# The third linear block turned by transfers and VectorE instead of TensorE, and three norms moved, in a two-layer sequence kernel on one Trainium2 core

## The chip, the cores and the metric

The kernel runs on one core of one Trainium2 chip. The metric is device time in microseconds (us) for one launch; lower is better. The kernel before takes 1119.91 us (median of three runs, 1119.85 to 1121.25). All times inside the run come from one profiled execution, which took 1119.75 us; its instructions span 1118.0 us. Engines have short names in the profile: PE is TensorE's matmuls, PEld its weight loads, DVE is VectorE, ACT ScalarE, POOL GpSimd, SP SyncE, which issues nearly all DMAs here. L770 is line 770 of the kernel before.

## The reference: what is computed

The input is 2 sequences of 1024 tokens, 512 wide. Four stages follow, each of the form "x = layernorm(x + f(x))" where f is, in turn, a Mamba layer (a selective state space with a short convolution and a gated RMS norm), a linear layer with ternary weights whose rows are rescaled by their norms, an RG-LRU (a gated linear recurrence with a short convolution), and a gated feed-forward network (SwiGLU) with integer weights. The two stages at which the change works come down to this:

```
# linear layer (L0_ffn)
out = einsum('bln,nk->blk', x, weight) * scale          # weight in {-1, 0, 1}
v   = max(norm(out), 1e-7)
out = out * tanh(v) / (v + 1e-7)
out = out * min(0.99 / max(norm(out), 1e-7), 1)

# RG-LRU (L1_attn)
y  = gelu(x @ w_y + b_y)
xb = x @ w_x + b_x
conv = conv_b + sum_k conv_w[k] * shift(xb, K - 1 - k)
gate_x, gate_a = sigmoid(conv @ w_ig + b_ig), sigmoid(conv @ w_ag + b_ag)
h = scan(exp(-8 * gate_a * softplus(a_param)), gate_x * conv * sqrt(1 - a * a))
out = (h * y) @ w_out + b_out
```

## The kernel before

**Tiling.** The 2048 tokens are four blocks of 512 tokens (block 0 to block 3, two to a sequence). A block's rows lie in X[b], 128 partitions by 4 rows of 512. A matmul needs its input with the features on the partitions, "turned". Two ways of turning are in the code:
- `transposed` (L226) does it on TensorE: for each of four feature pieces four transposes into one PSUM bank (L237), then a copy to SBUF. With `split` the copy is ScalarE's cast to a shorter float type (L241), and VectorE subtracts it from the original (L244), so that two matmuls on fast types give the exact product.
- `load_blocks` and `turn_blocks` (L260, L270) do it without TensorE: the rows are read back from DRAM by four DMAs that place 32 by 32 squares (256 KB each, in pieces of 128 bytes), and VectorE turns the squares in place, four instructions of 128x512 (L273). `split` (L939) then makes the two pieces, ScalarE's cast at L942 and VectorE's subtraction at L944.

**Stages on the time axis.** The Mamba layer runs over blocks 0 to 3 until about 450 us, the linear layer's blocks stand around 440 to 510 us, the RG-LRU follows to about 757, the feed-forward network to 1109, and the tail ends at 1118.

**Order of the work.** Stages are Python generators, and `weave` (L303) takes steps of a second generator between steps of the first by a written plan. `weave(branches(0, st), linear(2), (1,) * 4)` (L1174) thus mixes the first RG-LRU block's branch with the third linear block. The order on each engine follows from the emission and from a scheduler that may move instructions; `keep_in_program_order` and `high_priority` pin or hasten some, and `manual_schedule` fixes the tail as written. Each engine runs its queue strictly in that order.

**Mamba norms.** `conclude(b)` (L763) computes block b's output product (po, L770), adds it to the rows (L785), normalises them with `layernorm` (statistics L283 and L286 on VectorE, square root on ScalarE L288, reciprocal L289, then subtract and multiply L291 on VectorE or on GpSimd) and stores them to x_mid[b] in DRAM (`store_rows`, L257). conclude(b) is woven into block b+1's `project` and `recur` (L795 to L830). In recur, VectorE's scans (L578) produce what TensorE needs next.

**Linear layer.** `linear(b)` (L955): turned pieces, then for each of four row groups j a bank po of eight matmuls (L974), scaled on VectorE (L978), squared on ScalarE (L980), then a dozen operations on 128x4 elements (L984 to L996), the update of X[b] (L998, four instructions), and a `layernorm` on GpSimd with a store to x_lin[b]. Blocks 0 to 2 are turned by TensorE. Block 3 is turned from `mid`, which L1049 loads from x_mid[3]; the same block of code also loads X[3] and, in linear(3), the weights w14 of the RG-LRU's output.

**RG-LRU branch.** `branches(b)` (L1062): the turned block, then four channel groups m, each a product p (L1056) on TensorE, a padded copy xpad whose first three columns GpSimd clears (memset, L1079) or fills from the block before (L1081), ScalarE's bias add (L1082), VectorE's convolution (L1085 and three taps, L298); then four products for y with ScalarE's Gelu (L1093). xpad has two buffers, so channel group 2 waits for the convolution of group 0. `gates` (L1097) follows with eight more products.

**Tail.** The last block's four row groups are added up, normalised and stored one by one (L1305 to L1333). Row group 2 is normalised by two ScalarE passes (L1361, L1362) and stored from ScalarE's queue; row group 3 takes VectorE's statistics (L1364), a root on ScalarE (L1366), and is stored from SP.

Of the kernel before, what the change touches and what calls it, by code (L numbers as in the profile page):

```python
# [9 lines left out]
F32 = mybir.dt.float32  # L10
# [27 lines left out]
def model_kernel(ctx: ExitStack, tc: tile.TileContext, t: dict, out: bass.AP):  # L38
# [184 lines left out]
        nc.vector.tensor_scalar(r, z, 0.0, None, ALU.max)  # L223
        nc.vector.scalar_tensor_tensor(o, p, 2.0, r, ALU.mult, ALU.add)

    def transposed(pool, b, X, tags=("xT",), split=False, bufs=1, by_act=False, behind=False, soon=False):  # L226


        pieces = [
            pool.tile([P, NK, TB], F32R if split else F32, tag=tag, name=f"{tag}{b}", bufs=bufs)  # L230
            for tag in tags
        ]
        xT = pieces[0]
        for k in range(NK):
            pt = bank("pt")
            for j in range(NJ):
                nc.tensor.transpose(  # L237
                    pt[:, j * P : (j + 1) * P], X[b][:, j, k * P : (k + 1) * P], ident
                )
            if split:  # L240
                copied = nc.scalar.copy(xT[:, k, :], pt)  # L241
                if behind:
                    tc.keep_in_program_order(copied)
                nc.vector.tensor_tensor(  # L244
                    pieces[1][:, k, :], pt, xT[:, k, :].bitcast(F32), ALU.subtract
                )
            elif soon:
                with tc.high_priority():
                    nc.scalar.copy(xT[:, k, :], pt)
            elif k % 2 or by_act:  # L250
                nc.scalar.copy(xT[:, k, :], pt)
            else:
                nc.vector.tensor_copy(xT[:, k, :], pt)
        return pieces

    def store_rows(rows, x):
        nc.sync.dma_start(rows.rearrange("(j p) d -> p j d", p=P), x)  # L257
# [46 lines left out]
    def weave(main, fill, plan, rest=True):  # L304

        for i, _ in enumerate(main):
            for _ in range(plan[i] if i < len(plan) else 0):
                next(fill, None)
        for _ in fill if rest else ():
            pass  # L310
# [451 lines left out]
    def conclude(b, st):  # L762


        xc, sums = st["xc"], st["sums"]
        rms = sp.tile([P, NJ], F32, tag="rms", name="rms")
        for j in range(NJ):
            po = bank("po")
            for m in range(NX):
                nc.tensor.matmul(  # L770
                    po, xc[:, m, j * P : (j + 1) * P], w_out[:, m, :],
                    start=(m == 0), stop=(m == NX - 1),
                )
                if m == NX // 2 - 1:
                    yield
            if j == 0:
                pss = bank("pss")
                for i in range(NJ):
                    nc.tensor.matmul(
                        pss[:, i : i + 1], sums[:, i * P : (i + 1) * P], ones,  # L780
                        start=True, stop=True,
                    )
                nc.scalar.activation(rms, pss[:, :NJ], AF.Sqrt, bias=eps, scale=1.0 / DI)
                nc.vector.reciprocal(rms, rms)
            nc.vector.scalar_tensor_tensor(  # L785
                X[b][:, j, :], po, rms[:, j : j + 1], X[b][:, j, :], ALU.mult, ALU.add
            )
            yield
        layernorm(X[b])
        store_rows(x_mid[b], X[b])  # L790

    def by_blocks(b, st):

# [14 lines left out]
    for b in range(NBLK):  # L808
        if b:
            g, coming = gates(b, st), {}  # L810
            fill, plan = conclude(b - 1, before), (0, 0, 2, 0, 2, 0, 2, 2)
            ahead = iter(())
            if b + 1 < NBLK:
                by_blocks(b + 1, coming)
                ahead = head(b + 1, coming)
            weave(project(b, st), fill, plan, rest=False)

            weave(recur(b, H, st), alternate(itertools.chain(fill, g), ahead), (3,) * NJ)
        else:
            turns = (ahead, g, ahead, g, g, g, ahead)  # L820
            weave(recur(b, H, st), (next(steps, None) for steps in turns), (2, 2, 1, 2))
            for m in range(NX):
                tc.keep_in_program_order(nc.gpsimd.tensor_scalar(
                    w_out[:, m, :], w_out[:, m, :], normw[:, m : m + 1], 1.0, ALU.mult, ALU.mult
                ))
        H = st["H"]
        gate(b, st)
        before, st = st, coming
# [43 lines left out]
    def later_layers(exact, last=None):  # L872
# [82 lines left out]
        def linear(b):  # L955

            tags = ("wu0", "wd0") if exact else ("wu0",)
            if b == NBLK - 1:
                turn_blocks(mid)
                w1.append(wp.tile([P, NK, D], F32, tag="w4", name="w14" + suffix))  # L960
                xT = [ep.tile([P, NK, TB], WT, tag=tag, name=f"{tag}{b}") for tag in tags]
                split(mid, xT)
                nc.sync.dma_start(w1[4], w_sources["w_out"])
            else:

                xT = transposed(ep, b, X, tags=tags, split=exact, behind=b == 2)
            yield
            o = ep.tile([P, NJ, D], F32, tag="wF", name="o" + suffix)
            ssq = sp.tile([P, NJ], F32, tag="ssq", name="ssq")
            for j in range(NJ):  # L970
                po = bank("po")
                for k in range(NK):
                    for x in xT:
                        nc.tensor.matmul(  # L974
                            po, x[:, k, j * P : (j + 1) * P], wf[:, k, :],
                            start=(k == 0 and x is xT[0]), stop=(k == NK - 1 and x is xT[-1]),
                        )
                nc.vector.tensor_tensor(o[:, j, :], po, f0s, ALU.mult)  # L978
                junk = ep.tile([P, GW], mybir.dt.bfloat16, tag="junk", name="junk2")
                nc.scalar.activation(junk, o[:, j, :], AF.Square, accum_out=ssq[:, j : j + 1])  # L980
                if j % 2:
                    yield
            norm = sp.tile([P, NJ], F32, tag="norm", name="norm")
            nc.scalar.activation(norm, ssq, AF.Sqrt)  # L984
            v = sp.tile([P, NJ], F32, tag="v", name="v")
            nc.vector.tensor_scalar(v, norm, 1e-7, None, ALU.max)
            f = sp.tile([P, NJ], F32, tag="f", name="f")
            nc.scalar.activation(f, v, AF.Tanh)
            nc.vector.tensor_scalar(v, v, 1e-7, None, ALU.add)
            nc.vector.reciprocal(v, v)  # L990
            nc.vector.tensor_tensor(f, f, v, ALU.mult)
            nc.vector.tensor_tensor(norm, norm, f, ALU.mult)
            nc.vector.tensor_scalar(norm, norm, 1e-7, None, ALU.max)
            nc.vector.reciprocal(norm, norm)
            nc.vector.tensor_scalar(norm, norm, 0.99, 1.0, ALU.mult, ALU.min)
            nc.vector.tensor_tensor(f, f, norm, ALU.mult)  # L996
            for j in range(NJ):
                nc.vector.scalar_tensor_tensor(  # L998
                    X[b][:, j, :], o[:, j, :], f[:, j : j + 1], X[b][:, j, :],
                    ALU.mult, ALU.add,  # L1000
                )
            layernorm(X[b], engine=nc.gpsimd, last=None if b else nc.vector)
            if b:
                store_rows(x_lin[b], X[b])
            yield
# [39 lines left out]
        with tc.tile_pool(name="rec" + suffix, bufs=1, side="right", reuse_waits="tile") as rp:  # L1045
            carry = rp.tile([P, NK, 3], F32, tag="carry", name="carry1")
            last_h = rp.tile([P, NK], F32, tag="last", name="last")

            mid = rp.tile([P, NK, TB], F32, tag="xT", name="mid" + suffix)  # L1049
            load_blocks(mid, x_mid[3])  # L1050
            nc.sync.dma_start(X[3], rows_mid[3])

            def product(i, m, rhs):
# [117 lines left out]
                yield  # L1171

            st = {}
            weave(branches(0, st), linear(2), (1,) * 4)  # L1174
            lin = [coming_block(1)]
            bout = row("L1_attn_b_out", D, c1, nc.sync, "scale")
            ys = []
# [35 lines left out]
        with tc.tile_pool(name="ffn" + suffix, bufs=1, side="right", reuse_waits="tile") as fp:  # L1213
# [50 lines left out]
            for b in range(NBLK):  # L1264
# [29 lines left out]
                if final:  # L1294
# [37 lines left out]
                    def store(j, engine):  # L1332
                        engine.dma_start(xout[b][:, j, :], X[b][:, j, :])  # L1333
# [9 lines left out]
                    with tc.manual_schedule(  # L1343
# [13 lines left out]
                                store(j - 1, nc.sync)  # L1357
                        row_sum(3, False)
                        inverse(2)
                        x = X[b][:, 2, :]  # L1360
                        nc.scalar.activation(x, x, AF.Identity, bias=off[:, 2])  # L1361
                        nc.scalar.activation(x, x, AF.Identity, scale=rs[:, 2])  # L1362
                        row_st = sp.tile([P, 6], F32, tag="st", name="stf", bufs=4)
                        nc.vector.bn_stats(row_st, X[b][:, 3, :])  # L1364
                        nc.vector.bn_aggr(mean[:, 3, :], row_st)
                        nc.scalar.activation(rs[:, 3], mean[:, 3, 1:2], AF.Sqrt, bias=eps)  # L1366
                        store(2, nc.scalar)
                        inverse(3)
                        normed(3, nc.vector, mean[:, 3, 0:1], ALU.subtract)
                        store(3, nc.sync)  # L1370
                else:
                    for j in range(NJ):
                        r = fp.tile([P, D], F32, tag="r", name="r2", bufs=2)
# [60 lines left out]
```

## Time and profile before

| what | value |
|---|---|
| median of three runs | 1119.91 us (1119.85 to 1121.25) |
| profiled execution | 1119.75 us |
| its span | 1118.0 us |
| mean granted TensorE clock | 0.997 |
| 32 transposes, blocks 0 and 2 (L237, 458.27 to 461.76) | 3.49 us |
| one product of the RG-LRU (L1056) | 3.44 us |
| one normalisation on GpSimd, with subtraction (L291) | mean 2.17 us, 19 of them |
| one normalisation on VectorE (L291) | mean 0.57 us, 41 of them |
| four turns on VectorE (L273, 493.04) | 2.46 us |
| store of a block's rows to x_mid, issue to landing | 4.3 us (median) |

How to read it: the busy line gives for each engine its busy time, the share of the span and the number of instructions. A line of the waits gives an engine, its operation and line, what it waited for, and then the total, the number of times and the longest. A line of a timeline gives start, length, engine, line, operation, output and inputs, size and count, and in brackets the idle time before it with what ended it. Matmuls overlap, so their lengths are longer than their distance; the time of a group is read from start to the next start.

### The profile page before, as it was taken

The page shows a single profiled execution, that of the slowest core. Times are in us where ns is not written, and L with a number is a line of the kernel's source. Part 1 is how long each engine was busy: PE and PEld are TensorE (multiplying, and loading weights), DVE is VectorE, ACT ScalarE, POOL GpSimd, SP SyncE. Part 2 cuts the span into 40 slices and gives each one's busy share as a digit, 9 for nine tenths or more (in the row PEclk, how much of TensorE's full clock was granted, in tenths as well). Part 3 has the DMA queues.
Part 4 walks back from the last instruction along what each step waited for, and adds up shares of the span by engine and source line. Part 5 has one row for each costly group of instructions (what it writes and reads, how often), then busy time and mean ns, then how long its engine had stood idle before and what let it go on. Part 6 is the DMA issues. An engine that isn't in the chain of part 4 may idle for free.

```text
span 1118.0 us, 12076 instructions
## 1 busy us (share of the span) xinstructions
PE 1099.4 (98%) x4450; PEld 663.6 (59%) x4450; DVE 704.4 (63%) x1267; ACT 452.7 (40%) x692; POOL 364.5 (33%) x346
## 2 busy tenths in 40 slices
PE   9999999999999999999999999999999999999996
PEld 5455445445544555745444444447888888888885
DVE  5989797697869676874647438184238865325224
ACT  3334633463454233466654372553233224224223
POOL 1546471465248340273533231236411001001000
PEclk9999999999999999999999999999999999999998
DMA  8004202801220138336550001204654002100001
GB/s 323 21 9 122 94 1 92 207 0 38 88 98 0 39 124 226 67 94 153 111 76 25 13 1 44 32 0 138 192 95 76 1 1 62 15 1 32 6 1 41
DMA packets 122059, 77.04 MB, mean 69 GB/s; under 512 B 94512, under 2 KB 95312, under 8 KB 120456
## 3 DMA queue, kind: packets, MB, share of 16 engines
q1 hardware_dynamic: 120792, 75.77, 25.6%
q8 instruction: 37, 0.61, 0.2%
q10 hardware_dynamic: 976, 0.39, 0.1%
q14 instruction: 30, 0.25, 0.1%
q0 software_dynamic: 224, 0.02, 0.0%
HBM read 59.95 MB, written 16.02 MB: 68 GB/s over the span
## 4 chain that ended last, share of the span: by engine, by line
PE 81%; DVE 11%; ACT 4%; issue 1%; POOL 1%; DMA 1%; SPq 0%; DVEq 0%; ACTq 0%; POOLq 0%
PE pgu L1026 20%; PE p L1056 19%; PE po L1257 10%; PE pg L372 9%; PE px L372 7%; PE po L770 4%; DVE acc L298 3%; PE po L1146 2%; PE py L705 2%; PE po L974 2%; DVE L L578 2%; PE pxt L674 1%; PE pt L237 1%; DVE st L283 1%; POOL x L1152 1%
## 5 line engine op out<-in xcount | busy, mean ns | idle before, releaser
L1037 DVE SCALAR_TENSOR_TENSOR h<-pgu,L_ffn_up_scale,sg 128x512 f32<-128x512 f32 x63 | 47.1, 748 | 126.6 <-PE pgu L1026 122.8
L770 PE MATMUL po<-w_out,xc 128*128 128x512 f32 x256 | 112.5, 593 | 2.8 <-DVE L L578 2.8
L372 PE MATMUL px<-xT,w_in 128*128 128x512 f32 x256 | 114.6, 597 | 0.0
L593 POOL TENSOR_TENSOR L<-L,gm 128x512 f32<-128x512 f32 x64 | 93.4, 1490 | 64.8 <-DVE bdec L588 38.3
L372 PE MATMUL pg<-xT,w_in 128*128 128x512 f32 x256 | 113.5, 594 | 0.0
L1056 PE MATMUL p<-cv,w 128*128 128x512 f32 x256 | 110.8, 592 | 0.0
L1026 PE MATMUL pgu<-wF__4239,wg 128*128 128x512 f32 x256 | 101.7, 397 | 0.0
L1026 PE MATMUL pgu<-lo__4240,wg 128*128 128x512 f32 x256 | 100.8, 394 | 0.0
L1026 PE MATMUL pgu<-lo__4240,wu 128*128 128x512 f32 x256 | 100.7, 393 | 0.0
L1026 PE MATMUL pgu<-wF__4239,wu 128*128 128x512 f32 x256 | 100.7, 393 | 0.0
L1257 PE MATMUL po<-wd,hh 128*128 128x512 f32 x252 | 98.2, 396 | 0.3 <-POOL wg L917 0.3
L1257 PE MATMUL po<-wd,hl 128*128 128x512 f32 x252 | 98.2, 396 | 0.2 <-DVE hl L1041 0.2
L1036 ACT ACTIVATE sg<-pgu,L_ffn_gate_scale 128x512 f32<-128x512 f32 x63 | 43.4, 688 | 127.7 <-PE pgu L1026 127.6
L770 PEld LDWEIGHTS po<-w_out,xc 128*128 128x128 f32 x256 | 48.4, 190 | 63.8 <-issue 56.2
L1040 ACT CAST hh<-h 128x512 fp32r<-128x512 f32 x63 | 39.1, 620 | 112.5 <-DVE h L1037 112.3
L1056 PEld LDWEIGHTS p<-cv,w 128*128 128x128 f32 x256 | 48.6, 190 | 60.4 <-issue 59.1
L1056 PE MATMUL p<-xT,w 128*128 128x512 f32 x192 | 82.9, 592 | 0.0
L372 PEld LDWEIGHTS px<-xT,w_in 128*128 128x128 f32 x256 | 47.5, 190 | 57.5 <-issue 56.0
L372 PEld LDWEIGHTS pg<-xT,w_in 128*128 128x128 f32 x256 | 47.3, 190 | 54.2 <-issue 53.3
L1375 POOL TENSOR_TENSOR x<-x,r 128x512 f32<-128x512 f32 x12 | 15.1, 1291 | 195.2 <-DVE r L1374 195.2
L298 DVE SCALAR_TENSOR_TENSOR acc<-xpad,cols,acc 128x512 f32<-128x512 f32 x72 | 67.0, 933 | 18.5 <-ACT acc L342 13.8
L578 DVE TENSOR_TENSOR_SCAN L<-pl,id 128x512 f32<-128x512 f32 x64 | 74.9, 1205 | 4.5 <-ACT pl L572 3.5
(294 smaller groups left out, 1926.1 us busy)
## 6 DMA issues: line engine op xcount, KB each, us to landing
L<-decays SPq DMA_DIRECT2D x12, 1024.0 KB, 7.3
x_mid<-x SPq DMA_DIRECT2D x4, 1024.0 KB, 4.3
x<-x_mid SPq DMA_DIRECT2D x4, 1024.0 KB, 7.9
st<-in_L_ffn_gate_w_dram SPq DMA_DIRECT2D x8, 512.0 KB, 5.8
st<-in_L_ffn_up_w_dram SPq DMA_DIRECT2D x8, 512.0 KB, 4.1
st<-in_L_ffn_down_w_dram SPq DMA_DIRECT2D x8, 512.0 KB, 3.7
x_rec<-x SPq DMA_DIRECT2D x4, 1024.0 KB, 4.7
x<-_attn_hidden_states_dram SPq DMA_DIRECT2D x3, 1024.0 KB
```

Source lines behind the costliest of these rows:

```text
L298: tap = nc.vector.scalar_tensor_tensor(acc, xpad[:, k : k + TB], w[:, k : k + 1], acc, ALU.mult, ALU.add)
L372: nc.tensor.matmul(pm[:n, :], w_in[:, k, lo : lo + n], xT[:, k, :], start=(k == 0), stop=(k == NK - 1),)
L578: nc.vector.tensor_tensor_scan(L[:, h, :], pl, id4.rearrange("p j t -> p (j t)"), 0.0, ALU.mult, ALU.add)
L593: nc.gpsimd.tensor_tensor(L[:, h, :], L[:, h, :], st["gm"], ALU.mult)
L705: nc.tensor.matmul(pys[i][hh * HD : (hh + 1) * HD, q, :], dtx[q][:, 2 * i + hh, :], L[:, h, s], start=(first and q == 0), stop=(q == 1), s ...
L770: nc.tensor.matmul(po, xc[:, m, j * P : (j + 1) * P], w_out[:, m, :], start=(m == 0), stop=(m == NX - 1),)
L1026: nc.tensor.matmul(pm, w[g][:, k, cols], x[:, k, :], start=(k == 0 and x is pieces[0]), stop=(k == NK - 1 and x is pieces[-1]),)
L1036: nc.scalar.activation(sg, pgu[0], AF.Silu, scale=gs[:, m : m + 1])
L1037: nc.vector.scalar_tensor_tensor(h, pgu[1], us[:, m : m + 1], sg, ALU.mult, ALU.mult)
L1040: nc.scalar.copy(halves[0], h)
L1056: nc.tensor.matmul(pm, w1[i][:, k, m * P : (m + 1) * P], rhs[:, k, :], start=(k == 0), stop=(k == NK - 1),)
L1257: nc.tensor.matmul(po[j], x[:, j * P : (j + 1) * P], wd[m // GK][:, m % GK, :], start=(m == 0 and x is h[0]), stop=(m == NF - 1 and x is h ...
```

## The change

The diff has three parts.

1. linear(2) no longer uses `transposed`: like block 3 it is read back from x_mid[2] by four DMAs, turned by VectorE and split from SBUF. Both loads (mid[2] and mid[3]) are issued with high priority, and in the changed program's order their eight DMAs follow the store of x_mid[3] on SP. mid[2] takes a buffer of the tag "y". The weave's plan becomes (0, 0, 0, 0, 1, 0, 1, 1), so linear(2) starts after four steps more of branches(0), and the load of w14 moves from linear(3) to behind that weave.
2. Block 0's norm and store are taken out of conclude(0) and put into block 1's recur at its third chunk, with pinned statistics (`first_norm`, new). The last block's statistics are pinned too.
3. In the tail, row group 2 is normalised by one GpSimd instruction and stored from SP, and row group 3 is stored from ScalarE's queue.

```diff
             if split:
-                copied = nc.scalar.copy(xT[:, k, :], pt)
-                if behind:
-                    tc.keep_in_program_order(copied)
+                nc.scalar.copy(xT[:, k, :], pt)
...
-        layernorm(X[b])
-        store_rows(x_mid[b], X[b])
+        if b:
+            layernorm(X[b], pinned=b == NBLK - 1)
+            store_rows(x_mid[b], X[b])
+
+    def first_norm(chunks):
+
+
+        for c, _ in enumerate(chunks):
+            if c == 2:
+                layernorm(X[0], pinned=True)
+                store_rows(x_mid[0], X[0])
+            yield
...
-            weave(recur(b, H, st), alternate(itertools.chain(fill, g), ahead), (3,) * NJ)
+            chunks = recur(b, H, st)
+            if b == 1:
+                chunks = first_norm(chunks)
+            weave(chunks, alternate(itertools.chain(fill, g), ahead), (3,) * NJ)
...
-            if b == NBLK - 1:
-                turn_blocks(mid)
-                w1.append(wp.tile([P, NK, D], F32, tag="w4", name="w14" + suffix))
+            if b > 1:
+                turn_blocks(mid[b])
                 xT = [ep.tile([P, NK, TB], WT, tag=tag, name=f"{tag}{b}") for tag in tags]
-                split(mid, xT)
-                nc.sync.dma_start(w1[4], w_sources["w_out"])
+                split(mid[b], xT)
             else:
-
-                xT = transposed(ep, b, X, tags=tags, split=exact, behind=b == 2)
+                xT = transposed(ep, b, X, tags=tags, split=exact)
...
-            mid = rp.tile([P, NK, TB], F32, tag="xT", name="mid" + suffix)
-            load_blocks(mid, x_mid[3])
+            mid = {}
+            for b, tag, bufs in ((2, "y", 2), (3, "xT", 1)):
+                mid[b] = rp.tile([P, NK, TB], F32, tag=tag, name=f"mid{b}{suffix}", bufs=bufs)
+                with tc.high_priority():
+                    load_blocks(mid[b], x_mid[b])
             nc.sync.dma_start(X[3], rows_mid[3])
...
-            weave(branches(0, st), linear(2), (1,) * 4)
+            weave(branches(0, st), linear(2), (0, 0, 0, 0, 1, 0, 1, 1))
+            w1.append(wp.tile([P, NK, D], F32, tag="w4", name="w14" + suffix))
+            nc.sync.dma_start(w1[4], w_sources["w_out"])
...
-                        x = X[b][:, 2, :]
-                        nc.scalar.activation(x, x, AF.Identity, bias=off[:, 2])
-                        nc.scalar.activation(x, x, AF.Identity, scale=rs[:, 2])
+                        normed(2, nc.gpsimd, off[:, 2], ALU.add)
+                        store(2, nc.sync)
...
-                        store(2, nc.scalar)
                         inverse(3)
                         normed(3, nc.vector, mean[:, 3, 0:1], ALU.subtract)
-                        store(3, nc.sync)
+                        store(3, nc.scalar)
```

## The prediction

> **What bounds the kernel now.** I read the busy times first, then TensorE's list of waits, then the timelines of TensorE, VectorE, GpSimd and ScalarE from 444 to 505 us, and last the two other places that the change touches (134 to 145, 190 to 202, and the tail from 1108). Columns of a wait: us in total, times, longest.
>
> ```profile
> PE 1099.4 (98%) x4450; PEld 663.6 (59%) x4450; DVE 704.4 (63%) x1267; ACT 452.7 (40%) x692; POOL 364.5 (33%) x346
> ```
>
> ```profile
> PE po L770 <- DVE L L578: 2.8, 2, 1.9
> ...
> PE po L974 <- DVE wd L244: 0.8, 1, 0.8
> ```
>
> TensorE works 98% of the span and its waits add up to some 9 us, nearly all before 460. So whatever TensorE no longer does is gained in full, and any new wait is lost in full: behind it nothing has slack to give back (after 515 us its waits are 0.3 and 0.2). Two of the listed waits lie where the change works: 1.9 of the 2.8 at 143 us, and the 0.8 in the second block's linear product.
>
> **Part 1, the mamba norms.** Timeline of VectorE, then TensorE, in block 1 (start, length, engine):
>
> ```profile
> 137.11 0.68 DVE L283 BATCH_NORM_STATS2 st<-x 128x6 f32<-128x512 f32 x1
> 137.83 0.18 DVE L286 BATCH_NORM_AGGREGATE mv<-st 128x2 f32<-128x6 f32 x1
> 137.93 0.72 DVE L785 SCALAR_TENSOR_TENSOR x<-po,rms,x 128x512 f32<-128x512 f32 x1
> 138.68 0.69 DVE L283 BATCH_NORM_STATS2 st<-x 128x6 f32<-128x512 f32 x1
> 139.41 0.18 DVE L286 BATCH_NORM_AGGREGATE mv<-st 128x2 f32<-128x6 f32 x1
> 139.50 4.54 DVE L578 TENSOR_TENSOR_SCAN L<-pl,id 128x512 f32<-128x512 f32 x4
> ```
>
> ```profile
> 142.99 3.27 PE L770 MATMUL po<-w_out,xc 128*128 128x512 f32 x7 [1.95 <-DVE L L578]
> ```
>
> Block 0's statistics stand right ahead of the scans (L578) that TensorE then waits for. Two pairs of 0.82 leave that chain: 1.5 to 1.64 of the 1.95 go. They come back at 193 us, where VectorE stands idle for 3.51 us until 196.86. Four pairs (3.28) fit in; the reciprocal, two ScalarE table loads and four normalisations (1.95 us by the row at 456) do not all, and delay the gate chain from 198.18 by an estimated 1.15. VectorE then works without a gap from 226.6 to 258 and meets TensorE at 264.4 with about 0.3 to spare, so most of it is lost there. Net: −0.35 (ends −1.6, delay hidden, and +0.7, nothing won at 143). Two queues move with it: on SP the first store goes behind block 1's decays, and a load of block 3's rows behind it; no one waits for either before 240 us.
>
> The pinned statistics of the last block leave the place ahead of linear(1)'s subtractions (two of 0.67, at 449.14 and 449.80), and TensorE's wait of 0.79 at 451.74 goes, with about 0.2 of first-operand pacing: −0.97. Their cost comes later: block 3's rows are normalised at about 462.4 instead of 457.7, and the store follows.
>
> **Part 2, the transposes.** TensorE around linear(2):
>
> ```profile
> 458.27 3.65 PE L237 MATMUL pt<-ident,x 128*128 128x128 f32 x32
> 461.76 3.60 PE L1056 MATMUL p<-w,w 128*128 128x512 f32 x8
> ...
> 475.94 20.76 PE L1056 MATMUL p<-w,w 128*128 128x512 f32 x48
> ```
>
> 32 transposes take 3.49 us from start to start; half go: −1.75. A product of the recurrence takes 3.44 (20.6 us for 6). In the changed order six of them stand ahead of linear(2), so TensorE reaches linear(2) at 457.3 (linear(1)'s end) + 1.75 + 6 × 3.44 = 479.7, on the old clock.
>
> When is its operand there? It is now turned by VectorE, and the changed program puts those turns behind the convolutions of the first RG-LRU block and behind the turns of block 3. The convolutions' last two channels wait for a GpSimd memset (L1079), and in the new order both memsets stand behind linear(1)'s four normalisations; before, one stood ahead:
>
> ```profile
> 475.36 0.10 POOL L1079 MEMSET xpad<- 128x3 f32 x1 [1.40 <-DVE cv L298]
> 476.08 8.95 POOL L291 TENSOR_SCALAR x<-x,mv,rs 128x512 f32<-128x512 f32 x4 [0.62 <-DVE rs L289]
> 484.98 0.10 POOL L1079 MEMSET xpad<- 128x3 f32 x1
> ```
>
> and on VectorE (update, reciprocal, turns):
>
> ```profile
> 467.94 2.73 DVE L998 SCALAR_TENSOR_TENSOR x<-o,f,x 128x512 f32<-128x512 f32 x4
> ...
> 475.75 0.17 DVE L289 RECIPROCAL rs<-rs 128x4 f32<-128x4 f32 x1
> ...
> 493.04 2.46 DVE L273 STREAM_TRANSPOSE mid<-mid 128x512 f32<-128x512 f32 x4
> ```
>
> Step by step, with rows of before: ScalarE's four copies of block 0 end 2.65 behind 457.3; root (0.3), reciprocal and block 3's four normalisations (1.95) end at 462.4; linear(1)'s dozen small operations at 464.5; its update (2.73) at 467.2; four statistics pairs and the first convolution step at 470.5; table load 1.28, root and reciprocal, behind three taps, at 473.1. GpSimd: 4 × 2.07 (the shortest such row; VectorE then stands idle) to 481.4. Two convolutions (seven operations of about 0.68) to 486.2, block 3's turns (2.46) to 488.7, linear(2)'s first turn (0.62) and its cast (0.6) to 490.0. The subtractions wait for all four turns (491.1) and end at 493.9. TensorE by then has done 9 of linear(2)'s first 16 half-products (2.05) and a quarter of a product (0.86), and would have done so by 482.5: **stall 11.4**. The bounds: if the operations between take the shortest rows and taps overlap better, 8; with GpSimd at the 2.24 of the row above and transfers late by 2 us, 14.
>
> The transfers come second. All eight stand on SP behind block 3's store (4.3 us from issue to its completion by the rows of before), so they start at about 466.8. Before, 0.75 MB of such loads moved in 6.3 us (120 KB/us) and 1 MB of the later ones in 7 (140): 2 MB are there between 482 and 484, before VectorE gets to them. By themselves they would hold TensorE for 5 to 7 us.
>
> A GpSimd row is worth a second look: the same engine normalises in 0.77 in the tail where the first operation is an addition:
>
> ```profile
> 1109.36 0.77 POOL L1328 TENSOR_SCALAR x<-x,off,rsf 128x512 f32<-128x512 f32 x1 [0.72 <-DVE rsf L1325]
> ```
>
> The Trainium skill (GPSIMD Engine Reference, 3.1 Elementwise) counts 1.8 cycles an element at best, 769 ns for 512 elements. That agrees with L1328 and not with L291's 2.07 to 2.35, which stand for every normalisation that subtracts; by the page's figure the stall would be 5.2 shorter, about 6.
>
> **What an idle TensorE costs afterwards.** No row of before shows it idle for 10 us. The nearest is its own start: the 24 matmuls from 1.43 to 6.35, of the transposes' form, take 205 ns each where the later ones take 109.
>
> ```profile
> 1.43 4.92 PE L188 MATMUL early<-ident 128*128 128x128 f32 x24 [1.43 <-POOL ident masks.py:199]
> ```
>
> If it is slow again after the stall, the 2.7 us of work available from 490.1 to 493.9 need 2.7 × 205/109 = 5.1, which is 1.3 more than there is. Bounds: 0 and 24 × 96 ns = 2.3. I take 1.3, by the only row in which TensorE starts from idle.
>
> The Trainium skill (TensorE: Matmul & The Clock Gate, What's actually happening) says that the clock halves after an idle window of about 3.4 us and comes back after as much sustained work. By it the loss would be about 1.7, an estimate; the first rows agree in kind, though their column of the granted clock shows 1.00.
>
> **What follows the stall.** Everything later moves back by 8 to 9 us with TensorE. Linear(3)'s pieces are made while TensorE does the products in between; the gates' chain of block 1 needs GpSimd's squares, which by the rows end some 9 us ahead of need. I count nothing.
>
> **Part 3, the tail.**
>
> ```profile
> 1110.50 0.71 ACT L1361 ACTIVATE x<-x,off 128x512 f32<-128x512 f32 x1
> ...
> 1111.24 0.72 ACT L1362 ACTIVATE x<-x,rsf 128x512 f32<-128x512 f32 x1
> 1111.86 0.28 ACT L1366 ACTIVATE rsf<-mvf,eps 128x1 f32<-128x1 f32 x1
> ```
>
> The last row's root waits for ScalarE's two passes. The aggregate ends at 1111.61, so without them the root starts at 1111.63: −0.23. GpSimd's pass (0.77) ends at about 1111.6, beside this chain. The last store goes to ScalarE's queue: −0.25 in all (ends −0.5 and +0.2).
>
> **Sum**, against the profiled execution's 1119.75 (0.16 below the median of the runs shown, so nothing is corrected): −0.35 − 0.97 − 1.75 − 0.25 = −3.32, and + 11.4 + 1.3: **1129.1**.
>
> **Rivals.**
> A, the forecast: GpSimd's normalisations hold the convolutions, these hold the turns, TensorE stalls 10 to 13 us. For it: the waits of the changed program and the row of 8.95. 0.64; 1126 to 1131.
> B: GpSimd or the convolutions are quicker here, and the 2 MB behind the store decide. Stall 5 to 7, clock loss 0 to 1: 1116.4 + 6 + 0.5 = 1123. For it: rows of 0.77 for the same shape; against: 19 rows of L291 with a mean of 2.17. 0.18; 1121 to 1126.
> C, the other side: the operand is ready when TensorE gets there. It decides at 479.7: the first cast must have ended by then, so the transfers must end by 478.5 (2 MB in 11.7 us, 175 KB/us, where the rows give 120 to 140) and the turns must not sit behind the convolutions. Then only the gains remain: 1119.75 − 3.3 = 1116.4. For it: block 3's turned product at 503 us waits for nothing now. 0.07.
> D, nothing measurable: the stall is about 3 and eats the gains, 1118 to 1122; it needs both of B's and half of C's conditions. 0.05.
> E: the stall is longer, because the transfers share the engines with other loads, over 1132: 0.06.
>
> **How the numbers follow.** Faster and slower begin at 0.2%, 2.2 us, about what a measurement of this kernel can tell from no change. Faster is C, 0.07; same D, 0.05 and a little of B, 0.06; slower the rest, 0.87. The range takes in A and B and the unknown costs: 1121 to 1132.5.
>
> **What would show it.** In the profile after: a TensorE wait of about 10 us at L974's successor, ended by the cast of linear(2)'s first piece, with smaller ones by its subtractions; GpSimd's four normalisations ahead of two memsets; VectorE idle there until the memset; the 1.95 at 143 below 0.5; no wait in linear(1). If the wait ends by a transfer, it is B; if there is none, C. What would make me wrong most easily is an operation whose row does not hold at the new place, GpSimd's above all.

## The result and the profile after

| | time, us | against the kernel before (95% interval) |
|---|---|---|
| the changed kernel, median of 6 runs | 1128.89 (1128.24 to 1129.65) | 1.0073 (1.0062 to 1.0085) |
| the kernel before, beside it, 6 runs | 1120.58 (1119.73 to 1121.37) | |
| its profiled execution | 1128.88, span 1127.0 | span +9.0 |
| forecast | 1129.1, range 1121 to 1132.5 | |

The change makes the kernel 0.7% slower. The six runs of the kernel before fall into two groups, near 1119.8 and 1121.3, so times are compared by ratio to the kernel before on the same chip. From the linear layer on, the lines of after's code stand 8 to 13 further down, ahead of it 2 higher up: the linear layer's product is L982 (L974 before), its cast L953, its subtraction L955, the recurrence's product L1067, the memset L1090, the normalisation L289 (L291), the turn L271 (L273).

Busy times, then TensorE's waits, in the profile of the changed kernel:

```profile
PE 1099.9 (98%) x4434; PEld 663.0 (59%) x4434; DVE 707.6 (63%) x1271; ACT 450.5 (40%) x689; POOL 368.1 (33%) x347
```

```profile
PE po L982 <- ACT wu L953: 11.2, 1, 11.2
PE po L768 <- DVE L L576: 1.3, 2, 0.8
```

The busy share still reads 98%, and TensorE has 16 instructions fewer: these lines alone would not tell faster from slower. The waits do. The one of 1.95 at 143 us has shrunk to 0.49 (the sum of 2.8 became 1.3), linear(1)'s 0.8 is off the list, and a new one of 11.2 has come. The timeline of TensorE (start, length; in brackets the idle time before and what ended it):

```profile
141.55 2.84 PE L768 MATMUL po<-w_out,xc 128*128 128x512 f32 x6 [0.49 <-DVE L L576]
...
455.92 1.91 PE L237 MATMUL pt<-ident,x 128*128 128x128 f32 x16
457.66 1.88 PE L1067 MATMUL p<-w,w 128*128 128x512 f32 x4
...
489.63 1.22 PE L982 MATMUL po<-wfr,wu 128*128 128x512 f32 x2 [11.21 <-ACT wu L953]
490.65 1.91 PE L1067 MATMUL p<-w,w 128*128 128x512 f32 x2
491.57 1.41 PE L982 MATMUL po<-wfr,wd 128*128 128x512 f32 x1
```

Set against the lines of before: block 1's output product starts at 141.55 instead of 142.99 (−1.44); the transposes at 455.92 instead of 458.27 (another −0.91), and there are 16 of them, 1.74 us from start to start instead of 3.49 (−1.75). TensorE gets to linear(2) at 478.42 and starts it at 489.63. What follows runs late by a constant: the first gate products (gx) start at 505.94 instead of 496.54, +9.40. The span ends 9.05 later, so the tail gives −0.35.

What TensorE waits for is read upwards through GpSimd, VectorE and ScalarE:

```profile
471.46 9.75 POOL L289 TENSOR_SCALAR x<-x,mv,rs 128x512 f32<-128x512 f32 x4 [5.74 <-issue]
481.16 0.13 POOL L1090 MEMSET xpad<- 128x3 f32 x2
```

```profile
481.29 0.75 DVE L296 SCALAR_TENSOR_TENSOR cv<-xpad,cw,cv 128x512 f32<-128x512 f32 x1 [7.28 <-POOL xpad L1090]
...
482.42 3.52 DVE L296 SCALAR_TENSOR_TENSOR cv<-xpad,cw,cv 128x512 f32<-128x512 f32 x5
485.86 4.85 DVE L271 STREAM_TRANSPOSE mid<-mid 128x512 f32<-128x512 f32 x8
490.63 2.45 DVE L955 TENSOR_TENSOR wd<-mid,wu 128x512 fp32r<-128x512 f32 x4
```

Two memsets of three columns, 0.13 us together, stand behind 9.75 us of normalisation on GpSimd's queue. VectorE is idle 7.28 us for it, then does the two convolutions, then all eight turns (block 3's four first, so that block 2's first is the fifth), and the cast starts at 488.96, inside the turns. The chain of waits (start, us, what) names the same path:

```profile
475.03 6.18 POOL x L289 x3
481.22 0.09 POOL xpad L1090 x2
...
485.86 3.09 DVE mid L271 x5
488.96 0.63 ACT wu L953
489.63 1.22 PE po L982 x2
```

### The profile page after: what moved, and what is told of

Read it like the earlier page. It is cut to its first block, busy times and chain, and to the rows that moved or that the text cites. A ratio compares the mean times of both kernels' runs of the same rounds, so it can differ in the third digit from the quotient of the medians.

```text
span 1127.0 us, 12051 instructions
## 1 busy us (share of the span) xinstructions
PE 1099.9 (98%) x4434; PEld 663.0 (59%) x4434; DVE 707.6 (63%) x1271; ACT 450.5 (40%) x689; POOL 368.1 (33%) x347
## 4 chain that ended last, share of the span: by engine, by line
PE 82%; DVE 10%; ACT 3%; POOL 2%; issue 2%; DMA 1%; SPq 0%; DVEq 0%; ACTq 0%; POOLq 0%
PE pgu L1034 20%; PE p L1067 18%; PE po L1270 10%; PE pg L370 9%; PE px L370 7%; PE po L768 5%; PE po L982 3%; DVE acc L296 3%; PE po L1157 2%; PE py L703 2%; DVE L L576 2%; PE pxt L672 1%; POOL x L1163 1%; PE pt L237 1%; PE py L695 1%
## 5 line engine op out<-in xcount | busy, mean ns | idle before, releaser
L1067 PE MATMUL p<-cv,w 128*128 128x512 f32 x256 | 110.8, 592 | 0.0
L1067 PEld LDWEIGHTS p<-cv,w 128*128 128x128 f32 x256 | 48.6, 190 | 60.4 <-issue 58.8
L1067 PE MATMUL p<-xT,w 128*128 128x512 f32 x192 | 82.9, 592 | 0.0
```

Of the source, the lines that this page charges most:

```text
L1067: nc.tensor.matmul(pm, w1[i][:, k, m * P : (m + 1) * P], rhs[:, k, :], start=(k == 0), stop=(k == NK - 1),)
```

## The experiments

The **theory**: three gains of 4.1 us in all are kept, and one stall undoes them, made by GpSimd's normalisations ahead of the memset, with about a microsecond of slow clock behind it. The **rivals**: the transfers set the stall; the gains are lost again; the slow clock is no cost of its own. All ratios are to the kernel before on the same chip, with 95% intervals.

### The parts apart

**e1_norms_tail**: the norms' statistics and the tail as changed, linear(2) as before (the hunks of `transposed`, `linear`, the loads and the weave left out).

> The two moved norms, the pinned statistics and the tail alone; linear(2) stays with TensorE's transposes. My theory: the gains that the trace after shows in front of linear(2) stand by themselves: 1.44 us at the scans of block 1 and 0.9 in linear(1), and the tail gives 0.2 to 0.4. So 2.5 to 2.8 us under the kernel before, some 1117.6, with no TensorE wait over 1 us after 455. Rival: the later normalisation of block 3 holds linear(2)'s subtractions on VectorE, TensorE waits there for 1 to 2 us, and the gain shrinks to about 1.

Measured: 1117.54 us, 0.9972 (0.9961 to 0.9982), as the theory said. Norms and tail were not run apart; their shares are read from the traces.

**e2_turn_only**: the reverse, those hunks alone.

> Linear(2) by transfers alone; norms and tail as before. Here block 3 is normalised some 4 us sooner (its statistics stand ahead of linear(1) again), the eight transfers start sooner, and the built order has one of the two memsets ahead of GpSimd's normalisations. If the stall is set by GpSimd and the last convolution: it ends about 489, 8 to 9 us of waiting, and the time is 1128 to 1129, as the whole change. If the parts simply add: 1128.9 + 2.7 = 1131.6. If the transfers set it: 4 us shorter than in the whole change, 1124 to 1125.

Measured: 1131.31 us, 1.0089 (1.0072 to 1.0106), and a stall of 10.2. The parts add up: the first takes 2.6 us off, the second adds 11.2, and the whole change adds 8.3. So the moved norms are a gain of their own. My 1128 to 1129 for e2 was too low: GpSimd's normalisations start at 477.12, later than I guessed, and the second memset comes at 486.45. In this profile 1.7 us of the lateness arise long before linear(2): behind the wait at 143 us the granted clock is 0.50 from 143.6 to 146.9, where the kernel before shows 1.00, and linear(1)'s transposes start at 449.80 instead of 448.12.

### What holds the operand

**e3_memset_on_vector**: block 0's padding cleared by VectorE.

```diff
-                        nc.gpsimd.memset(xpad[:, 0:3], 0.0)
+                        (nc.vector if b == 0 else nc.gpsimd).memset(xpad[:, 0:3], 0.0)
```

> The changed kernel with the memsets of the first block's padded copies on VectorE, so that its convolutions no longer wait for GpSimd's four normalisations. If GpSimd alone set the stall (the forecast's theory): the convolutions end near 478 instead of 485.9, and the stall falls by 7 to 8 us, to about 1121. If the transfers were nearly as late: the last of the eight was issued at 477.8 and took about 7, so it landed near 485; VectorE then waits for it, and the gain is 1 us at most, 1128.

Measured: 1125.16 us, 1.0044 (1.0027 to 1.006), stall 7.0. VectorE in this kernel:

```profile
475.80 3.87 DVE L296 SCALAR_TENSOR_TENSOR cv<-xpad,cw,cv 128x512 f32<-128x512 f32 x5
481.11 4.86 DVE L271 STREAM_TRANSPOSE mid<-mid 128x512 f32<-128x512 f32 x8 [1.44 <-DMA mid<-x_mid]
```

The convolutions no longer wait, and the turns start 4.75 us earlier, now held by the transfers. The time lies between the two expected ones: GpSimd's queue was the cause of 4.2 us of the stall, and 7.0 are left. Of these VectorE waits 1.44 for the transfers, and block 3's four turns, ahead of block 2's, take 2.4; the remaining 3.2 are its own chain.

**e6_gpsimd_add_form**: GpSimd adds a negated mean instead of subtracting the mean; its order is untouched.

```diff
+        if engine is nc.gpsimd:
+            less = sp.tile([P, NJ, 1], F32, tag="less", name="less")
+            nc.vector.tensor_scalar(less[:, :n], mv[:, :n, 0:1], -1.0, None, ALU.mult)
...
+            if by is nc.gpsimd:
+                by.tensor_scalar(
+                    x[:, j, :], x[:, j, :], less[:, j, :], rs[:, j, :], ALU.add, ALU.mult
+                )
...
```

> The changed kernel, but every GpSimd normalisation adds the negated mean instead of subtracting the mean, with one small VectorE operation for the sign. If it is the subtraction that makes them 2.1 to 2.4 us where the tail's take 0.77: the four of them take 3.1, the memsets come 6 us sooner, the transfers set the rest as in the run with the memsets on VectorE, and the time is about 1125. If it is the place or the operands: no change, 1128.9.

Measured: 1126.53 us, 1.0055 (1.0038 to 1.0072), stall 7.9. The groups of the changed kernel and of this one (count, busy us, mean ns of one; last the engine's idle time before them and what ended it):

```profile
L289 POOL TENSOR_SCALAR x<-x,mv,rs 128x512 f32<-128x512 f32 x19 | 41.0, 2172 | 45.0 <-PE pt L237 32.0 <-DVE rs L287 7.3 <-issue 5.7
```

```profile
L294 POOL TENSOR_SCALAR x<-x,less,rs 128x512 f32<-128x512 f32 x19 | 17.9, 951 | 42.6 <-PE pt L237 31.9 <-DVE rs L287 5.5 <-issue 5.1
```

Same shape, same engine, same count: 2172 ns with a subtraction first, 951 with an addition (the operand is another tile too; g1 and g2 below part the two). The four ahead of the memset take 5.25 instead of 9.75, and here too the turns then wait for the transfers (they start at 481.96). Two different ways of freeing the memset thus end at the same second limit, with 1.44 and 1.73 us of waiting for transfers.

### The clock

**e7_tensor_kept_busy**: 40 matmuls, read by nothing (extra work), fill TensorE's wait.

```diff
+            if b == 2:
+                fill = bank("fill")
+                for _ in range(40):
+                    tc.keep_in_program_order(nc.tensor.matmul(
+                        fill, wf[:, 0, :P], wf[:, 0, :], start=True, stop=True
+                    ))
```

> The changed kernel with 40 matmuls on the ternary weights alone in TensorE's queue ahead of linear(2), about 9.1 us into a bank that nobody reads, so that TensorE is idle for some 2 us instead of 11. The operand comes when it came. If the idle time costs clock afterwards: linear(2)'s first matmuls run at full speed, and the time is 1.3 to 2.3 us under the changed kernel, 1127. If the slow start has another cause: the same time, 1128.9.

Measured: 1128.07 us, 1.0067 (1.0051 to 1.0084). Windows of the changed kernel, then of this one: busy time of PE, PEld, DVE, ACT and POOL, the granted clock, the DMA share (it can exceed 1), GB/s.

```profile
480.00:488.00 8.00, 0.00 (x0) 0.00 (x0) 6.67 (x11) 0.00 (x0) 2.86 (x7) 0.73 1.11 236
488.00:492.00 4.00, 2.37 (x5) 1.49 (x5) 4.00 (x8) 2.40 (x4) 0.00 (x0) 0.50 1.11 232
492.00:496.00 4.00, 4.00 (x14) 2.97 (x13) 1.78 (x3) 0.38 (x1) 0.00 (x0) 0.76 1.07 99
```

```profile
488.00:492.00 4.00, 2.27 (x7) 1.05 (x7) 4.00 (x8) 2.40 (x4) 0.00 (x0) 1.00 1.11 190
492.00:496.00 4.00, 4.00 (x16) 2.57 (x16) 2.45 (x4) 0.72 (x2) 0.00 (x0) 1.00 0.71 66
```

The operand is there at the same time (linear(2) starts at 489.62 and 489.63), but the clock stays at 1.00, linear(2)'s second row group starts at 497.25 instead of 498.45, and the first gate products at 504.73 instead of 505.94. In the two traces the slow clock costs 1.2 us. The times agree in sign only: 1128.07 against 1128.89, 0.0006 in the ratios, with intervals that overlap, and 1127 was expected. The 0.76 is a mean: the clock was 0.50 until 493.9 and 1.00 from there. The remaining 1.1 us behind the wait (9.40 late, and 4.10 of gains undone, make 13.5; the wait is 11.2 and the clock 1.2 of it) stay with a full clock. There the subtractions pace TensorE: in e7 linear(2)'s first wd products start at 491.32, 491.92, 492.53 and 493.13, 0.6 us apart, later ones 0.46, and a subtraction takes 0.61 (four in 2.45).

### The transfers, and the queue they stand in

**e9_load_early**: mid[2] loaded as soon as its rows are stored, into the buffer "lo"; the turns pinned behind the convolutions.

```diff
+        mid = {2: ep.tile([P, NK, TB], F32, tag="lo", name="mid2" + suffix)}
+        load_blocks(mid[2], x_mid[2])
...
-                turn_blocks(mid[b])
+                turn_blocks(mid[b], pinned=b == 2)
...
```

> The changed kernel with block 2's four loads issued right after the parameters, long before the store of block 3, into a buffer of their own; block 2's turns stay behind the convolutions, which still wait for GpSimd, but now stand ahead of block 3's turns. If GpSimd and the convolutions set the stall: only the four turns ahead (2.45 us) go, the stall is about 8.7 and the time 1126.4. If the transfers set it: no TensorE wait is left but 1 to 2 us, 1118 to 1119.

Measured: 1143.27 us, 1.0199 (1.0182 to 1.0216). TensorE's waits, and SP's queue:

```profile
PE p L1067 <- DVE xT L271: 13.7, 1, 13.7
PE po L984 <- ACT wu L955: 8.8, 1, 8.8
```

```profile
481.79 0.51 SPq L1062 DMA_DIRECT2D x<-x_mid  x1
504.80 0.37 SPq L1187 DMA_DIRECT2D w<-in_L_attn_w_out_dram  x1
505.28 4.39 SPq L263 DMA_DIRECT2D lin<-x_lin  x2
```

The stall at linear(2) is 8.8 (8.7 was forecast). With the operand's transfers early, the turns start at 485.99 as before, still behind GpSimd's queue; the 2.4 us come from block 3's turns, which now stand behind block 2's. So the two limits overlap and neither is removed alone. The time is 16.9 us above the 1126.4 expected, most of it the 13.7, a wait I had not foreseen. On SP the load of w14 waits until 504.80 for a product that still reads its buffer, and the loads of the next block's rows stand behind it.

**e4_load_and_turn_early**: mid[2] early, its turns ahead of the convolutions, and the next block's loads put ahead of w14.

> The changed kernel with block 2's four loads issued behind the parameters into a buffer of their own, and the loads of the next block's rows issued ahead of the RG-LRU's output weights; in the built order block 2's turns now stand ahead of linear(1)'s update and of the convolutions. Then the operand waits for neither the eight transfers nor GpSimd. My theory: it is there at about 467, TensorE gets to it at 478.4 and does not wait; all of the change's gains are left: 1120.1 - 2.6 (norms and tail) - 1.75 (transposes) = 1115.8. Rival: VectorE's added 5 us (turns, subtractions) ahead of the convolutions come back later as a wait for the convolutions at the gates, 2 to 4 us, and the time is 1118 to 1120.

Measured: 1131.57 us, 1.0097 (1.008 to 1.0114), a miss of 16 us. Linear(2) waits for nothing now, but the waits have moved:

```profile
PE p L1067 <- DVE xT L271: 8.3, 1, 8.3
PE po L984 <- DVE wd L957: 3.7, 1, 3.7
```

```profile
490.06 3.15 SPq L263 DMA_DIRECT2D lin<-x_lin  x2
517.32 0.36 SPq L255 DMA_DIRECT2D x_lin<-x  x1
517.72 4.16 SPq L263 DMA_DIRECT2D lin<-x_lin  x2
```

Two of the four loads are issued at 490. Then a store that waits for GpSimd's next norm takes its turn, and the other two leave at 517.72. It is the same shape as the memset: something that could go stands behind something that waits, on another queue.

**e10_both_limits_off**: the memset on VectorE, mid[2] early, turns behind the convolutions, the next block's loads ahead of w14.

> The memsets on VectorE and block 2's loads early, but the turns kept behind the convolutions (and now ahead of block 3's), with the same place of the output weights. If GpSimd's memsets and the transfers are the only two limits: the convolutions end near 478 to 480, the first piece is cast at about 480 to 481 and TensorE waits 2 to 3 us instead of 11.2, with no loss of clock: about 1118.5. If VectorE itself is a third limit just behind them: 5 us or more of waiting, 1121 or more.

Measured: 1125.23 us, 1.004 (1.0028 to 1.0053), and not 1118.5. Linear(2)'s stall is 3.2 (2 to 3 forecast), the 3.2 that e3 left to VectorE's own chain, whose turns now start at 480.21 without a gap before them. 3.1 more come from the same place on SP (last two loads at 525.12). And no loss of clock was expected, but the granted clock is 0.50 from 480.5 to 487.3: the first gate products start at 498.70, in f1 below, without a stall, at 492.43. Of these 6.3 us only 3.2 are the wait; the rest is slow clock and pacing, which this run does not part. So behind this stall of 3.2 us as much was lost again.

### A version without the stall, and why it does not win

**f1_no_stall**: the whole change with the memset on VectorE, mid[2] loaded early and turned ahead of the convolutions by the plan (1, 0, 0, 0, 1, 0, 1), the next block's rows in a buffer of their own ("y") ahead of w14, and GpSimd's norms adding. Beside it **f2_norms_tail_again**, which is e1 once more.

> The whole change with every wait found so far taken away: block 2's loads early into a buffer of their own use, its turns ahead of the convolutions (plan 1, 0, 0, 0, 1, 0, 1), the next block's rows loaded into the buffer that block 2's had, ahead of the output weights, GpSimd's normalisations in the adding form, the memsets on VectorE. By the rows of the runs so far, no TensorE wait over 1 us is left between 455 and 560; then the transposes' 1.75 us is at last gained: 1117.5 - 1.75 + 0.7 of small waits at linear(3) = 1116.5, about 1 us under the norms and tail alone. If VectorE's 5 us of turns and subtractions find a place that is bound after all, it is no faster than those, 1117.5 or more.

> The norms and the tail alone, on the same chip as the run with all waits taken away: 1117.5 as before, 0.28% under the kernel before. The difference of the two is what the turn by transfers is worth when nothing waits for it: 1 us less there by my theory, none or the other sign by the rival's.

Measured: f1 1117.78 us, 0.9984 (0.9975 to 0.9993); f2 1116.93 us, 0.9977 (0.9967 to 0.9986). f1 was to take 1116.5 and missed it. No wait above 0.3 is left around linear(2) in f1, and the turn by VectorE does save TensorE time. From the transposes behind linear(1) to the first gate product TensorE takes 36.53 us in f1 and 38.27 in e1 and f2, 1.74 less; to the first product of the feed-forward network 277.77 against 279.09 and 279.05, 1.3 less. But f1 lost 1.2 us in the feed-forward stage, which the change does not touch. By the chain of waits, the time from the stage's first seven output products to its last 14 is 337.56 in e6 and 337.59 in f1, and 336.32 to 336.48 in the ten other traces (the expectations below count 2.3 us more into the stage). Only those two kernels have the new 16-byte tile `less`. Saving and loss leave the two spans alike (medians 1115.2 for f1, 1115.1 for f2); the rest of the 0.85 us between the times lies outside the span of the instructions, and no run explains it.

**g1_no_stall_no_new_tile** writes the negated mean over the mean; **g2_new_tile_alone** is e1 with the tile added and written, and read by nothing (GpSimd subtracts).

The edit of g1, against f1:

```diff
-            less = sp.tile([P, NJ, 1], F32, tag="less", name="less")
-            nc.vector.tensor_scalar(less[:, :n], mv[:, :n, 0:1], -1.0, None, ALU.mult)
+            nc.vector.tensor_scalar(mv[:, :n, 0:1], mv[:, :n, 0:1], -1.0, None, ALU.mult)
```

> The kernel without any wait (f1_no_stall) is 0.7 us ahead of the one with the norms and the tail alone at the end of the recurrence, and loses 1.2 us in the feed-forward stage, whose time from the first to the last product is 339.85 us instead of 338.7. Both kernels with that longer stage have a new tile of 16 bytes a partition for the negated mean, and GpSimd adds in its norms. Here the negated mean is written over the mean, so no tile is new and nothing in SBUF moves, while GpSimd still adds. Theory (the new tile moves the later tiles and costs the 1.2): feed-forward stage 338.7, time some 0.7 below that of the norms and the tail alone. Rival (the quicker norms, or something else that f1 changes, cost it): stage 339.85, time some 0.5 to 0.9 above it.

> The norms and the tail alone (the best version so far), with the 16-byte tile added and written, but read by nothing: GpSimd subtracts as before. This is some extra work, five small VectorE operations. Theory (the tile's place costs it): feed-forward stage 339.85 us, time 1.1 above the best version, so about 1118.5 beside a kernel before of 1119.9. Rival (the tile costs nothing): stage 338.7, time as the best version, 0.9972 to 0.9977 of the kernel before.

Measured: g1 1117.98 us, 0.9979 (0.9969 to 0.9988), feed-forward stage 336.39; g2 1118.86 us, 0.9982 (0.9973 to 0.9991), stage 337.60. The stage follows the tile in all four cases, as the theory said. The same 48 matmuls late in it, by the chain of waits of g1 and of g2:

```profile
1086.85 11.15 PE pgu L1040 x48
```

```profile
1089.89 11.20 PE pgu L1042 x48
```

Each matmul takes some 1 ns longer (0.05 us over 48), and the stage has some 1450. That the tile's presence costs it is shown; that it does so by moving the later tiles to other addresses is only argued, since no other size or place of a tile was run.

The two runs also part e6's rivals. g1 reads the mean's own tile and adds, 1059 ns a normalisation; g2 has the new tile and subtracts, 2246 ns. So it is the operation, not the operand.

On time g1 missed; it was to be 0.7 us below the norms and the tail alone. Its last normalisation ends at 1109.30, 0.90 ahead of f2's 1110.20, but its span ends 6.7 us after that, f2's 4.9. The last store has moved by 1112. VectorE's two closing synchronisations (DRAIN) start at 1113.2 and 1115.6 in g1, at 1114.0 and 1114.6 in f2: 1.8 us more go by between them, while the other engines have theirs behind them by 1113.9. The only packets of g1 after 1112.5 are three on an instruction queue, two of them between 1113.7 and 1114.3, so a load of code is a suspect; no run tests it, and the cause stays open. f1, f2, g1 and g2 all come out under the kernel before, the norms and the tail alone lowest (e1 and f2, 0.9972 and 0.9977), with g1's 0.9979 not told from them. The turn by transfers and VectorE, freed of every wait, saves TensorE 1.3 us by 735 us, but was not shown to lower the time.

## Why the prediction was right

Rival A came true. Its terms against the trace (the stall is the wait of 11.2 and the 1.1 of pacing by the subtractions, which the working counted into it):

| step | forecast, us | measured, us |
|---|---|---|
| block 1's statistics moved | −0.35 | −1.44 |
| linear(1)'s wait | −0.97 | −0.91 |
| 16 transposes | −1.75 | −1.75 |
| stall, with the pacing by the subtractions | +11.4 | +12.3 |
| slow clock behind it | +1.3 | +1.2 |
| tail | −0.25 | −0.35 |
| profiled execution | 1129.1 | 1128.88 |

The mechanism was right. That the total is right to 0.2 us is luck: 1.1 us more gain at block 1 and 0.9 more stall cancel.

**What bounds the kernel** held. Every wait that left TensorE's list before 460 us was gained in full, and of the 13.5 us lost at linear(2) nothing was made up.

**The stall** was right by its chain and 0.9 us too short. The working stands on the old clock, so block 1's 1.44 has to come off its times. TensorE was then to be there at 478.3 and was at 478.42; GpSimd's norms were to begin at 471.7 and began at 471.46. But they took 2.44 each, where the working had taken the shortest row, 2.07, and ended at 481.2 instead of 480.0. The turns began at 485.86 (484.8 forecast) and the cast at 488.96 (488.0).

**The mis-sized term** is the moved statistics of block 0. I had the norm delay the gate chain by 1.15 and lose most of the 1.6 by 264 us. VectorE in block 1 of the changed kernel:

```profile
191.84 0.67 DVE L281 BATCH_NORM_STATS2 st<-x 128x6 f32<-128x512 f32 x1
...
195.75 1.91 DVE L289 TENSOR_SCALAR x<-x,mv,rs 128x512 f32<-128x512 f32 x4
197.57 0.75 DVE L734 TENSOR_TENSOR xc<-xc,py 128x256 f32<-128x256 f32 x2
```

TensorE is 1.44 ahead here, and the gate chain starts at 197.57 where before it started at 198.18, only 0.61 earlier. So the norm did delay it, by 0.83 (1.15 forecast). What failed is the next step, that VectorE meets TensorE at 264 us with the delay still on it. VectorE before, then after:

```profile
246.36 1.11 DVE L588 TENSOR_TENSOR bdec<-L,tk 128x256 f32<-128x256 f32 x1
...
264.26 1.27 DVE L676 TENSOR_TENSOR dtx<-pxt,tk 128x512 f32<-128x512 f32 x2
```

```profile
245.57 0.40 DVE L586 TENSOR_TENSOR bdec<-L,tk 128x256 f32<-128x256 f32 x1
...
262.81 1.28 DVE L674 TENSOR_TENSOR dtx<-pxt,tk 128x512 f32<-128x512 f32 x2
```

One operation that takes 1.11 us before takes 0.40 after. These 0.71 make up most of the delay, and at 264 VectorE is 1.45 ahead, like TensorE. Its neighbours of the same shape take 0.42 and 0.41 before too (231.34, 239.45); why this one took longer no run shows. The gain is still whole at 446.68 (448.12 before).

**The clock** was right in kind and size: 1.3 from the only row in which TensorE starts from idle, 1.2 by e7's trace. The size holds for this stall; in e10 a wait of 3.2 was followed by some 3 us of slow clock and pacing.

**Rival B** was wrong as a forecast and right as a second limit. With GpSimd out of the way the turns waited for the transfers until 481.1 (e3) and 482.0 (e6), where the working, less 1.44, has 480.6 to 482.6. The stall was then 7.0 and 7.9, at and above the upper end of B's 5 to 7, though only 1.44 and 1.73 of it was VectorE waiting for transfers. In the changed kernel they hide behind the memset. "What follows the stall: I count nothing" held: after 500 us no wait of TensorE is above 0.3 until the feed-forward stage.

**GpSimd's rate.** With a subtraction first the changed kernel shows 2172 ns, so the row of before decided rightly; with an addition first e6 shows 951. The Trainium skill (GPSIMD Engine Reference, 3.1 Elementwise) gives 1.8 cycles an element at best, 769 ns for 512, and does not tell the two apart there. The tail's additions agree (770 ns); no subtraction here comes near it.

On the clock, the changed kernel was granted 0.50 from 483.65, 5.2 us after its last product, and e10 from 480.5, 2.1 us after it. The Trainium skill (TensorE: Matmul & The Clock Gate, What's actually happening) has the clock halve after an idle window of some 3.4 us. The first agrees; e10, whose whole wait was 3.2 us, does not, and there the measurement decides.

## What to carry to other kernels

When work leaves the engine that sets the time, follow its replacement through every queue that it now stands in: here 0.13 us of memsets behind 9.75 us of norms cost more (4.2 us by e3) than the 1.75 us of transposes that the change saved. Take each limit away singly and then together, since a second one may lie right behind the first, and on a DMA queue look for the store or load that waits, and what stands behind it. A stall costs more than its length when TensorE's clock drops with it. Time a stage that nobody touched as well: a small new tile can slow it.

## What the runs showed of the hardware

- GpSimd's normalisation of 128x512 takes 2169 to 2246 ns with a subtraction first (before, after, e1, g2) and 951 to 1085 ns with an addition first (e6, f1, g1), means over 19 each.
- The granted clock fell to 0.50 in the changed kernel 5.2 us after the last product and came back 4.3 us after the restart, at 493.9; filling the wait (e7) won 1.2 us in the trace. In e10, with a wait of 3.2 us, it fell after 2.1 us and came back 5.7 us after the restart.
- Loads that stood on SP's queue behind one that waits cost TensorE 13.7 us (e9) and 8.3 us (e4).
- A 16-byte tile made a later stage of matmuls 1.2 us (0.36%) longer, in all three kernels that have it (e6, f1, g2), also where nothing reads it (g2); its mechanism stays open.
